# An attention and expert block on one core: turning the column maxima between two value tiles, with their result in another PSUM bank

## The chip, the cores and the metric

The kernel runs on one core of a Trainium2 chip. The metric is the device time of one execution in microseconds (us). Lower is better. Engines are named as in the profile: PE is the matrix engine, PEld its weight loads, DVE the vector engine, ACT the scalar engine, POOL the GpSimd engine, SP the engine that issues most DMAs.

## The reference, cut to what matters

```
h = layernorm(x) * (1 + ca) + sa            # x: 8 batches x 1024 rows x 256
q, k, v = h @ w_qkv                         # 16 heads of 64
attn = softmax(q @ k.T / 8, axis=-1)        # over 1024 keys, per head
x = x + ga * concat(attn @ v) @ w_o
h = layernorm(x) * (1 + cb) + sb
x = x + gb * moe(h)                         # 8 experts, 512 rows each by top-k
```

The factors sa, ca, ga, sb, cb, gb come from a small product with a conditioning vector. The change lies in the softmax of the attention: in how the maximum of the scores over the keys is found and passed on.

## The kernel before

Attention takes the first 3190 us of the span. It is cut into 128 **units** (`NSU`): a batch, a pair of heads and a half of the 1024 queries (512). A unit has 1024 keys in eight **chunks** of 128. Scores are computed transposed: keys lie on partitions, and the two heads' 512 queries each lie side by side (128 x 1024).

The loop over `g` runs four **groups** a unit (`u, gm = divmod(g, 4)`), two chunks in a group, and the instructions of each engine run in the order in which the loop writes them (`manual_schedule`). Three units are under way at once. In group g the loop writes

- `subtract` (L432, DVE): adds the negated maximum, spread over partitions by `max_spread` (L429), to two chunks of an earlier unit;
- `scores_mm` and `scores_out`: PE writes the scores of two chunks of unit u (L373), ACT copies each to SBUF (L382), DVE keeps the running maximum over chunks in `top` (L387). In the last group (`gm == 3`) one of the two subtractions comes behind these;
- the tasks "m1": projections of queries, keys (`qk_task`, L338) or values (`v_task`, L355) for later units, and at the first group of a unit `max_rows` (L416, L421);
- `exp_of` (L435, ACT), then `values_mm` for two chunks of an earlier unit (L444, PE; the group's **two value tiles**), whose sums build up in one bank over the unit's eight chunks, and `add_up` (L460, L463, POOL) for the denominators;
- in the last group `max_turn` and `split_max`: PE turns `top` in eight transposes (L394) into the tile `tt`; DVE reduces `tt` to the negated maxima (L402) and splits these into three bf16 parts in four small operations (L407 to L410), which `max_rows` turns back;
- the tasks "m2", among them the **small tasks** of the next and the previous batch: layernorm transposes, output projections, transposes of their rows.

[...] `ps_s` has two buffers of two banks each, for scores and for `tt`; they are handed out in turn, so in a last group and the next one the order is chunk 6, chunk 7, `tt`, next unit's chunk 0, its chunk 1. `ps_b` (two banks) holds the spread maximum, `ps_av` (one) the values, and `ps_m` (one, tag "mm") every projection and small task. At the very beginning `bank` hands out other banks for projections as well.

The small tasks are given groups by `free_slot`, which enters them in `taken`; with `behind` it takes last groups only:

```
def free_slot(g, behind=False):
    while g in taken or g % 4 == 0 or behind != (g % 4 == 3):
        g += 1
    taken.add(g)
```

From these calls 112 of the 128 last groups are claimed. Free are those of groups 3, 7, ... 35 (units 0 to 8) and 55, 59, ... 79 (units 13 to 19). All of them hold one "m1" task: a projection of queries or of values. In group 3 there are no value tiles yet, and `mod_rows` is written behind the turn, though it has no entry in `taken`.

Of the kernel before, what the change touches and what calls it, by code (L numbers as in the profile page):

```python
# [28 lines left out]
F32 = mybir.dt.float32  # L29
# [9 lines left out]
P = 128  # L39
# [4 lines left out]
def adaln_block(  # L44
# [77 lines left out]
    NSU = B * NP * 2  # L122
# [11 lines left out]
    ps_m = attn.enter_context(tc.tile_pool(name="ps_m", bufs=1, space=PSUM))  # L134
# [110 lines left out]
    tops, turned, rows_of, less, probs, sums, avs = {}, {}, {}, {}, {}, {}, {}  # L245
# [6 lines left out]
    def run(g, where):  # L252
        for f, args in steps.pop((g, where), ()):
            f(*args)
# [108 lines left out]
    def unit(u):  # L363
        return u // (2 * NP), u // 2 % NP, u % 2

    def scores_mm(u, c):

        b, p, h = unit(u)
        qt, kt = qks[b, p, 0], qks[b, p, 1]
        ps = ps_s.tile([P, 2, QB], F32, tag="s", name=f"s{u}_{c}")  # L370
        for j in range(2):
            r = slice(j * N, (j + 1) * N)
            nc.tensor.matmul(  # L373
                ps[:, j, :], kt[r, c * P : (c + 1) * P], qt[r, h * QB : (h + 1) * QB],
                start=True, stop=True,
            )
        return ps

    def scores_out(u, c, ps):

        probs[u, c] = work.tile([P, 2, QB], F32, tag="p", name=f"p{u}_{c}", bufs=PB)
        nc.scalar.copy(probs[u, c], ps)  # L382
        if c == 0:
            return
        if c == 1:
            tops[u] = work.tile([P, 2, QB], F32, tag="top", name=f"top{u}", bufs=1)
        nc.vector.tensor_tensor(tops[u], probs[u, 0] if c == 1 else tops[u], ps, ALU.max)  # L387

    def max_turn(u):
        top = tops.pop(u)  # L390
        turned[u] = ps_s.tile([P, 8, P], F32, tag="s", name=f"tt{u}")
        for j in range(2):
            for t in range(4):
                nc.tensor.transpose(  # L394
                    turned[u][:, 4 * j + t, :], top[:, j, t * P : (t + 1) * P], ident
                )

    def split_max(u):

        tt = turned.pop(u)  # L400
        nm = tt[:, :2, :8]
        nc.vector.tensor_reduce(nm[:, 0, :], tt, AX.X, ALU.max, negate=True)  # L402
        part = [
            parts_of[u % 2][:, :, :, i].rearrange("p t j -> p j t") for i in range(3)
        ]
        whole, rest = (nm[:, i, :].rearrange("p (j t) -> p j t", j=2) for i in range(2))
        nc.vector.tensor_copy(part[0], whole)  # L407
        nc.vector.tensor_sub(rest, whole, part[0])
        nc.vector.tensor_copy(part[1], rest)
        nc.vector.tensor_sub(part[2], rest, part[1])  # L410
# [12 lines left out]
    def max_spread(u):  # L423

        less[u] = ps_b.tile([P, 2, QB], F32, tag="less", name=f"less{u}")
        rows = rows_of.pop(u)
        for j in range(2):
            r = slice(j * N, (j + 1) * N)
            nc.tensor.matmul(less[u][:, j, :], three[r, :], rows[r, :], start=True, stop=True)  # L429

    def subtract(u, c):
        nc.vector.tensor_tensor(probs[u, c], probs[u, c], less[u], ALU.add)  # L432

    def exp_of(u, c):
        nc.scalar.activation(probs[u, c], probs[u, c], AF.Exp)  # L435

    def values_mm(u, c):
        b, p, h = unit(u)
        if c == 0:
            avs[u] = ps_av.tile([P, QB], F32, tag="av", name=f"av{u}")  # L440
        v, pT = vs[b, p // 2], probs[u, c]
        for j in range(2):
            hh = 2 * (p % 2) + j
            nc.tensor.matmul(  # L444
                avs[u][j * N : (j + 1) * N, :], v[:, c, hh * N : (hh + 1) * N], pT[:, j, :],
                start=(c == 0), stop=(c == NT - 1),
            )

    def values_out(u):
        b, p, h = unit(u)  # L450
        if h == 0:
            oTs[b, p] = work.tile([P, S], F32, tag="oT", name=f"oT{b}_{p}", bufs=2)
        nc.scalar.copy(oTs[b, p][:, h * QB : (h + 1) * QB], avs.pop(u))  # L453

    def add_up(u, i):

        pts = [probs.pop((u, 2 * i + k)) for k in range(2)]
        if i == 0:
            sums[u] = work.tile([P, 2, QB], F32, tag="acc", name=f"acc{u}")
            nc.gpsimd.tensor_tensor(sums[u], pts[0], pts[1], ALU.add)  # L460
        else:
            for pt in pts:
                nc.gpsimd.tensor_tensor(sums[u], sums[u], pt, ALU.add)  # L463
# [236 lines left out]
    taken = set()  # L700
# [5 lines that stand above are left out]
        return g  # L706
# [9 lines left out]
    for b in range(B):  # L716
# [16 lines left out]
        if b + 1 < B:  # L733
# [3 lines left out]
            for t in range(NT):  # L737
                g = free_slot(64 * (b + 1) + 19 + 4 * t, True)
# [3 lines left out]
                if t % 2:  # L742
                    g = free_slot(g + 2, True)
                    at(g, "m2", out_turn, ps_m, b, t - 1)
                    g = free_slot(g + 1)
                    at(g, "m2", out_route, ps_m, b, t - 1)
                    at(g + 1, "post", out_exp, b, t - 1)
                    g = g + 2 if g + 2 < 4 * NSU else 4 * NSU + 4
# [17 lines left out]
    with tc.manual_schedule():  # L766
# [20 lines left out]
        g = -1  # L787
        while g < 4 * NSU + LAG or steps:
            u, gm = divmod(g, 4)
            run(g, "load")  # L790
            if gm == 1 and 0 < u <= NSU:
                max_spread(u - 1)
            u1, gm1 = divmod(g - LAG + 1, 4)
            late = [(u1, 2 * gm1 + i) for i in range(2) if 0 <= u1 < NSU]

            for uc in late[: 1 if gm == 3 else 2]:
                subtract(*uc)
            if 0 <= u < NSU:
                for c in (2 * gm, 2 * gm + 1):
                    scores_out(u, c, scores_mm(u, c))  # L800
            if gm == 3 and late:
                subtract(*late[1])
            run(g, "m1")
            run(g, "post")
            for uc in late:
                exp_of(*uc)
            u1, gm1 = divmod(g - LAG, 4)
            if 0 <= u1 < NSU:
                for c in (2 * gm1, 2 * gm1 + 1):
                    values_mm(u1, c)  # L810
                if gm1 == 3:
                    values_out(u1)
                if u1 < NSU - 1 or gm1 < 2:
                    add_up(u1, gm1)
            if gm == 3 and 0 <= u < NSU:
                max_turn(u)
                split_max(u)
            run(g, "pool")
            run(g, "m2")
            g += 1  # L820
# [117 lines left out]
    with tc.tile_pool(name="search", bufs=2) as se, tc.tile_pool(  # L938
        name="pos", bufs=1
    ) as po_, tc.tile_pool(name="se_ps", bufs=2, space=PSUM) as sps, tc.tile_pool(  # L940
        name="pos_ps", bufs=1, space=PSUM
# [280 lines left out]
```

## Time and profile before

| | us |
|---|---|
| median of 3 runs (3564.46 to 3565.72) | 3565.45 |
| the profiled execution, its own time | 3568.2 |
| its span, first to last instruction | 3566.5 |
| PE busy in the span | 3435.0 |
| DVE, POOL, ACT busy in the span | 2864.9, 2657.6, 2439.2 |
| L394, turned maxima: 1024 matmuls on PE | 139.9 |
| L402, the reduction: 128 of 1.23 us each | 157.4 |
| L407 to L410, the split: 128 of each, of 0.17 to 0.19 us | 96.7 |

Busy times are sums over the span, whose parts have different limits. PE matmuls overlap, and their ends are modelled, so times on PE are better read from start to start. In the lines of a timeline the columns are start, length, engine, line, operation, output and inputs, shapes and number; brackets hold the idle time ahead and what ended it. In the lines of a table of stretches busy times of PE, PEld, DVE, ACT and POOL follow the length, and then the granted PE clock, the DMA share and GB/s. In the lines of waits the numbers are the total in us, how often, and the longest.

### The profile page before, as it was taken

Reading aid. Unit: us, or ns where it says so; the run is one execution under the profiler, and the core shown is the slowest. Engines: PE = TensorE matmul, PEld = TensorE weight load, DVE = VectorE, ACT = ScalarE, POOL = GpSimd, SP = SyncE. Lnnn points to the kernel's source line nnn. Section 1 sums busy time; section 2 is a strip of 40 time slices with the busy share of each in tenths; the row PEclk is TensorE's granted clock in tenths of the full one; section 3 lists DMA queues with packets and bytes.
Section 4 is the critical chain, followed back from the end, with each engine's and each line's share of the span. In section 5 each row is a group of like instructions: output and inputs, shape, how many; then the busy total and the mean of one; then the engine's idle time right before and its main releaser. Section 6 shows DMA issues by size and latency. Waiting matters only on the chain. (4 is left out here: it accounts for less than half of the span.)

```text
span 3566.5 us, 54197 instructions
## 1 busy us (share of the span) xinstructions
PE 3435.0 (96%) x20631; PEld 1444.8 (41%) x20631; DVE 2864.9 (80%) x3611; ACT 2439.2 (68%) x2996; POOL 2657.6 (75%) x1533
## 2 busy tenths in 40 slices
PE   8999999999999999999999999999999999993898
PEld 3333334343433434344333444334433343432566
DVE  6888888888888888888888888888888888887332
ACT  5777777777777777777777777777777777760111
POOL 2778777888888887988788877978788888881233
PEclk9999999999999999999999999999999999996899
DMA  4021012011120112111221112011211112124342
GB/s 78 13 42 31 25 40 60 29 46 46 55 56 29 50 58 56 34 40 46 63 48 35 50 52 64 25 43 45 65 52 31 47 51 57 46 80 151 94 103 42
DMA packets 190136, 185.39 MB, mean 52 GB/s; under 512 B 49308, under 2 KB 167596, under 8 KB 189748
## 3 DMA queue, kind: packets, MB, share of 16 engines
q1 hardware_dynamic: 173916, 160.54, 16.6%
q0 software_dynamic: 7168, 12.72, 1.8%
q10 hardware_dynamic: 8792, 8.67, 0.8%
q8 instruction: 162, 2.65, 0.3%
q14 instruction: 98, 0.80, 0.1%
HBM read 127.06 MB, written 63.21 MB: 53 GB/s over the span
## 5 line engine op out<-in xcount | busy, mean ns | idle before, releaser
L463 POOL TENSOR_TENSOR acc<-acc,p 128x1024 f32<-128x1024 f32 x764 | 1811.3, 2371 | 360.7 <-ACT p L435 327.5
L382 ACT COPY p<-s 128x1024 f32<-128x1024 f32 x1024 | 996.3, 1019 | 417.3 <-PE s L373 406.4
L432 DVE TENSOR_TENSOR p<-p,less 128x1024 f32<-128x1024 f32 x1024 | 1206.7, 1210 | 32.8 <-PE less L429 30.3
L387 DVE TENSOR_TENSOR top<-top,s 128x1024 f32<-128x1024 f32 x768 | 936.8, 1220 | 268.6 <-ACT p L382 228.4
L435 ACT ACTIVATE p<-p 128x1024 f32<-128x1024 f32 x1024 | 1041.7, 1057 | 73.0 <-DVE p L432 72.8
L373 PE MATMUL s<-qk,qk 64*128 64x512 f32 x4096 | 1024.3, 612 | 34.2 <-DVE parts L410 31.1
L444 PE MATMUL av<-p,v 128*64 128x512 f32 x4096 | 965.8, 592 | 1.8 <-ACT oT L453 1.8
L373 PEld LDWEIGHTS s<-qk,qk 64*128 64x128 f32 x4096 | 358.4, 186 | 527.1 <-issue 240.4
L338 PE MATMUL pq<-hT,wq 128*64 128x512 f32 x2048 | 498.4, 608 | 2.2 <-ACT hT L303 2.2
L444 PEld LDWEIGHTS av<-p,v 128*64 128x64 f32 x4096 | 281.0, 137 | 462.4 <-issue 365.8
L460 POOL TENSOR_TENSOR acc<-p,p 128x1024 f32<-128x1024 f32 x128 | 304.3, 2377 | 170.6 <-ACT p L435 170.6
L338 PEld LDWEIGHTS pq<-hT,wq 128*64 128x64 f32 x2048 | 125.2, 136 | 341.5 <-issue 210.8
L355 PE MATMUL pv<-wq,hT 128*64 128x256 f32 x2048 | 249.2, 385 | 0.0
L1142 ACT ACTIVATE h<-ph,b_sb 128x512 f32<-128x512 f32 (+1 forms) x72 | 46.1, 640 | 254.1 <-PE ph L1138 254.1
L402 DVE TENSOR_REDUCE tt<-tt 128x8 f32<-128x1024 f32 x128 | 157.4, 1230 | 68.8 <-PE tt L394 68.7
L580 PE MATMUL po<-wo,ot 128*64 128x256 f32 x1792 | 205.7, 382 | 0.0
L355 PEld LDWEIGHTS pv<-wq,hT 128*64 128x64 f32 x2048 | 135.7, 136 | 152.3 <-issue 66.5
L387 DVE TENSOR_TENSOR top<-p,s 128x1024 f32<-128x1024 f32 x128 | 155.8, 1217 | 15.0 <-ACT p L382 15.0
L394 PEld LDWEIGHTS tt<-ident,top 128*128 128x128 f32 x1024 | 109.6, 140 | 106.4 <-DVE top L387 106.4
L525 POOL TENSOR_TENSOR oT<-oT,rb 128x1024 f32<-128x1024 f32 x63 | 151.0, 2398 | 0.0
L580 PEld LDWEIGHTS po<-wo,ot 128*64 128x64 f32 x1792 | 123.6, 137 | 66.1 <-issue 9.4
L394 PE MATMUL tt<-ident,top 128*128 128x128 f32 x1024 | 139.9, 280 | 2.3 <-DVE top L387 2.3
(180 smaller groups left out, 2271.0 us busy)
## 6 DMA issues: line engine op xcount, KB each, us to landing
rb<-rden_d SPq DMA_DIRECT2D x126, 256.0 KB
oT_d<-oT SPq DMA_DIRECT2D x62, 512.0 KB
ot<-oT_d SPq DMA_DIRECT2D x56, 512.0 KB
rows_d<-row SPq DMA_DIRECT2D x64, 132.0 KB
rows_d<-gb_d SPq DMA_DIRECT2D x8, 1024.0 KB
w<-in_L_ffn_w_dram ACTq DMA_DIRECT2D x8, 1024.0 KB
w<-in_L_ffn_w_dram SPq DMA_DIRECT2D x8, 1024.0 KB
lnx<-in_L_attn_inputs_dram SPq DMA_DIRECT2D x28, 256.0 KB
```

Of the source, the lines that this page charges most:

```text
L338: nc.tensor.matmul(pq[m * N : (m + 1) * N, :], wq_of(k, a, 2 * p + m), hTs[b][:, k, sl], start=(k == 0), stop=(k == KC - 1),)
L355: nc.tensor.matmul(pv[m * N : (m + 1) * N, i, :], hTs[b][:, k, t0 : t0 + N], wq_of(k, 2, 4 * g, 4), start=(k == 0), stop=(k == KC - 1),)
L373: nc.tensor.matmul(ps[:, j, :], kt[r, c * P : (c + 1) * P], qt[r, h * QB : (h + 1) * QB], start=True, stop=True,)
L382: nc.scalar.copy(probs[u, c], ps)
L387: nc.vector.tensor_tensor(tops[u], probs[u, 0] if c == 1 else tops[u], ps, ALU.max)
L394: nc.tensor.transpose(turned[u][:, 4 * j + t, :], top[:, j, t * P : (t + 1) * P], ident)
L432: nc.vector.tensor_tensor(probs[u, c], probs[u, c], less[u], ALU.add)
L435: nc.scalar.activation(probs[u, c], probs[u, c], AF.Exp)
L444: nc.tensor.matmul(avs[u][j * N : (j + 1) * N, :], v[:, c, hh * N : (hh + 1) * N], pT[:, j, :], start=(c == 0), stop=(c == NT - 1),)
L460: nc.gpsimd.tensor_tensor(sums[u], pts[0], pts[1], ALU.add)
L463: nc.gpsimd.tensor_tensor(sums[u], sums[u], pt, ALU.add)
L580: nc.tensor.matmul(po[m * N : (m + 1) * N, :], ot[:, p, m * N : (m + 1) * N], wo[:, p, :], start=(p == 0), stop=(p == NP - 1),)
```

## The change

In the last groups that no small task has claimed, `max_turn` is written between the two value tiles instead of behind both, and `split_max` puts the negated maxima and their remainders into a tile of their own in the bank "mm", no longer into a corner of `tt`. In all other last groups the order and the tiles are as they were. In group 3 only the second part applies, since there are no value tiles.

```diff
-    def split_max(u):
+    def split_max(u, apart):
         tt = turned.pop(u)
-        nm = tt[:, :2, :8]
+        if apart:
+            nm = ps_m.tile([P, 2, 8], F32, tag="mm", name=f"nm{u}")
+        else:
+            nm = tt[:, :2, :8]
         nc.vector.tensor_reduce(nm[:, 0, :], tt, AX.X, ALU.max, negate=True)
...
             u1, gm1 = divmod(g - LAG, 4)
+            turn = gm == 3 and 0 <= u < NSU
+            alone = turn and g not in taken
             if 0 <= u1 < NSU:
                 for c in (2 * gm1, 2 * gm1 + 1):
+                    if alone and c % 2:
+                        max_turn(u)
                     values_mm(u1, c)
                 if gm1 == 3:
                     values_out(u1)
                 if u1 < NSU - 1 or gm1 < 2:
                     add_up(u1, gm1)
-            if gm == 3 and 0 <= u < NSU:
-                max_turn(u)
-                split_max(u)
+            if turn:
+                if u not in turned:
+                    max_turn(u)
+                split_max(u, alone)
             run(g, "pool")
             run(g, "m2")
```

## The prediction

> **What bounds the kernel now.** I read the page's busy shares and slices first, then the table of stretches for the granted clock, then the waits of PE, then the timeline of one affected group on PE, DVE and ACT.
>
> ```profile
> PE 3435.0 (96%) x20631; PEld 1444.8 (41%) x20631; DVE 2864.9 (80%) x3611; ACT 2439.2 (68%) x2996; POOL 2657.6 (75%) x1533
> 66.00:257.00 191.00, 181.00 (x986) 66.74 (x984) 159.28 (x169) 147.92 (x177) 143.37 (x65) 1.00 0.12 26
> 520.00:1000.00 480.00, 477.97 (x2921) 193.75 (x2919) 408.20 (x494) 356.20 (x435) 391.68 (x222) 1.00 0.19 48
> PE s L373 <- DVE parts L410: 31.1, 70, 1.3
> ```
>
> PE is busy 96% of the span, and in attention (to 3170 us) it is the engine that sets the pace: from 520 to 1000 us it rests 2 us in 480. From 66 to 257 us it rests 10 us in 191, at the same granted clock of 1.00, and the list of waits for that stretch gives all 10.0 us to one cause: scores (L373) waiting for the last instruction of the split (L410). Over the whole kernel that wait is 31.1 us in 70 times. Fifteen of these are 1.25 us each (units 1 to 8 and 13 to 19 in the timeline), 18.8 us together; the other 55 are about 0.2 us.
>
> Here is one of the fifteen, unit 19, on PE, then on DVE, then on ACT (start, length, instruction):
>
> ```profile
> 492.26 1.95 PE L355 MATMUL pv<-wq,hT 128*64 128x256 f32 x16
> 494.03 1.89 PE L444 MATMUL av<-p,v 128*64 128x512 f32 x8
> 495.85 1.10 PE L394 MATMUL tt<-ident,top 128*128 128x128 f32 x8
> 496.88 1.13 PE L373 MATMUL s<-qk,qk 64*128 64x512 f32 x4
> 499.26 1.13 PE L373 MATMUL s<-qk,qk 64*128 64x512 f32 x4 [1.25 <-DVE parts L410]
> 500.32 0.41 PE L416 MATMUL pn<-ident_b,parts 128*64 128x128 bf16 x8
> ```
>
> ```profile
> 492.62 2.55 DVE L387 TENSOR_TENSOR top<-top,s 128x1024 f32<-128x1024 f32 x2 [1.79 <-ACT p L382]
> 495.08 1.22 DVE L432 TENSOR_TENSOR p<-p,less 128x1024 f32<-128x1024 f32 x1
> 496.98 1.23 DVE L402 TENSOR_REDUCE tt<-tt 128x8 f32<-128x1024 f32 x1 [0.69 <-PE tt L394]
> ...
> 498.92 0.19 DVE L410 TENSOR_TENSOR parts<-tt,parts 128x8 bf16<-128x8 f32 x1
> ```
>
> ```profile
> 491.57 1.93 ACT L382 COPY p<-s 128x1024 f32<-128x1024 f32 x2 [0.34 <-PE s L373]
> 494.25 0.59 ACT L360 COPY v<-pv 128x512 f32<-128x512 f32 x1 [0.75 <-PE pv L355]
> ```
>
> The two score buffers rotate: chunk 6, chunk 7, turned maxima (tt), next unit's chunk 0, its chunk 1. So chunk 1 needs the buffer of tt, and the negated maxima lie in that same buffer until L410 has read them. L410 ends at 499.11, chunk 1 starts 0.15 later. PE has only chunk 0 to do meanwhile.
>
> **What the Trainium skill says.** "PSUM — Partial Sum Buffer", section "PSUM bank collisions raise a hardware error", asks to guard PSUM by bank and quadrant, not by address, readers of two engines included. The trace agrees twice: chunk 1 stays out until the small operations on a corner of the tile are over, and the maximum of chunk 6 starts at 492.62, just as the ACT copy of the same tile ends (491.57 plus half of the pair, about 492.6). The same page, "Engine vs sequencer instructions", says that matmuls start and complete in program order; so an early turn that waits holds the second value tile. "TensorE: Matmul & The Clock Gate", section "HAM oscillation — how this bites in real kernels", puts the danger at PE gaps above some 3.4 us. Here gaps are 1.25 us and the clock is 1.00 with or without them: closing them brings no clock, and I count none.
>
> **The change part by part.** It acts in 16 last groups: those that `free_slot` leaves free, groups 3 to 35 and 55 to 79. Group 3 (unit 0) has no value tiles yet, and the second modulation product follows its turn; the trace has no stall there, so it counts zero. Fifteen remain.
>
> *Stall removed.* Price it by starts, not by the reported idle: from chunk 0 to the bank transposes L416 is 500.32 − 496.88 = 3.44 us. Without a wait two chunks take 1.92 us, as in this row pair of unit 20, whose last group has an output projection as cover:
>
> ```profile
> 524.20 1.99 PE L373 MATMUL s<-qk,qk 64*128 64x512 f32 x8
> 526.12 0.41 PE L416 MATMUL pn<-ident_b,parts 128*64 128x128 bf16 x8
> ```
>
> So the stall costs 1.52 us (1.25 reported, the rest start-up of a matmul after a wait). Spacing says the same: affected units are 23.72 us apart, unit 20 takes 25.82 with a projection of 3.60, that is 22.22, or 1.50 less. The fifteen are worth 15 × 1.52 = 22.8 us.
>
> *New wait.* The turn moves ahead of the second value tile. The first ends half of 1.82 us after 494.03, at 494.94. The column maxima are ready when the pair at 492.62 ends, 495.17. From there to a waiting turn it takes 0.06 us, by the last unit, where that wait exists already:
>
> ```profile
> 3177.65 2.54 DVE L387 TENSOR_TENSOR top<-top,s 128x1024 f32<-128x1024 f32 x2
> 3180.25 1.09 PE L394 MATMUL tt<-ident,top 128*128 128x128 f32 x8 [0.59 <-DVE top L387]
> ```
>
> Turn at 495.23, PE loses 0.29 us; what is queued behind it is the second value tile, the next scores and so all of PE. Unit 18 gives the same (468.88 + 2.55 + 0.06 against 470.29 + 0.91), unit 1 gives 0.23. This cannot shrink by a lighter DVE: DVE idled 1.79 us ahead of that maximum, which hangs on the ACT copy and that on PE's own scores.
>
> *Does the stall really go?* Turn 495.23 to 496.25 (pitch 1.02), second value tile to 497.16, chunk 0 to 498.12. The reduction starts 1.13 after the turn as before, 496.36, when the addition L432 before it is just over (495.08 + 1.22 = 496.30), and ends 497.59. Plus 0.15 that is 497.74, ahead of 498.12 by 0.38. Chunk 1 doesn't wait. The split ends 3.26 us after the turn starts, as now (499.11 − 495.85), so at 498.49; the transposes L416 now come at 499.08, so they don't wait either.
>
> *The maxima in the small tasks' bank.* The reduction needs that bank free: its last user in these groups is pq or pv, copied out by ACT by 494.84 (unit 19), 1.5 us before. Next user is L416's output, which needs the split anyway. Same five DVE operations, input and output in PSUM as now, so I price them unchanged. The trace has no reduction into another bank; I bound it by nothing below and by the 0.38 us of slack above, past which it would show one for one.
>
> *A turn between two tiles that accumulate.* No row shows it. Value tiles after pv, pq or the bf16 transposes all take 1.82 a pair, so I take 0; ends −0.05 and +0.10 (what a restart costs chunk 1 now: pitch 1.06 instead of 0.96).
>
> *Behind it.* All later steps come 1.23 us earlier. ACT has 0.16 us to spare ahead of the chunk 2 copy and may slip 0.02; that copy frees nothing that PE needs for 4 us. DVE is busy 159.28 us in 8 units, 19.9 each, POOL 17.9, ACT 18.5, all under the new 22.5 of PE. No DMA is moved; SP and POOL keep their order.
>
> Sum: 22.8 − (14 × 0.29 + 0.23) = 18.5 us. The profiled execution took 3568.2 (span 3566.5) and goes to 3549.7; the median shown is 2.75 under that execution, so 3565.45 becomes **3547.0**. The bounds of the unknown terms give 13 to 21 us, 3544.5 to 3552.5.
>
> **Rivals.**
> *Held to the end (9%).* The buffer is still given back only after L410, say because the release counts the whole split. Then chunk 1 starts at 498.49 + 0.15 = 498.64 instead of 498.12, with 0.10 restart: 0.62 lost. Gain 1.52 − 0.29 − 0.62 = 0.61, times 15 is 9.2: 3556.3. Against it: the only later readers use the new tile.
> *Given back (7%).* ACT, whose slack is the smallest, or DVE with 2.6 us a unit, turns the gain into a later wait of about 0.9 us a unit; left is 5 us, 3560.5. Against it: the 520 to 1000 stretch runs at 22.2 plus tasks with the same DVE work.
> *Slower (4%): the bank of the small tasks holds the reduction.* It stands at the head of DVE's queue, with the four small operations, two additions and the next maximum behind it, and all of PE behind these. It decides from the point where the ACT copy of pq or pv ends after 496.36 + 0.38 + 1.23 − 0.10 = 497.87, 3.0 us later than now. If the copy came only behind the next unit's chunk 0 copy (498.11 + 1.01 + 0.59 = 499.7), chunk 1 would start at 501.1, 1.8 us later than today: +27 us, 3592. Against it: ACT idles 0.75 us ahead of that copy.
> *It doesn't do what it says (2%).* Another set of groups is touched and the stalls stay: 3565. For the fifteen speaks that exactly those without a claimed slot stall 1.25 us.
>
> **How the numbers follow.** The forecast itself has 78%. Its own span 3544 to 3552.5 holds about 75 in 100; reaching to the first rival, 3556.5, takes in 8 in 10 and a little more. Faster or slower means by more than 0.2% (7 us), about what a measurement of this kernel can tell from no change: faster are the forecast, the first rival and a part of the second, 0.90; same 0.06; slower 0.04.
>
> **What would show it.** Right: "scores waiting for L410" falls from 31.1 to about 12 us with 0.2 the longest; a new wait of turn for column maxima of about 0.2 to 0.3 us in 15 places; affected units 22.5 apart; DVE's idle ahead of the reduction near 0.1 there. Wrong: waits of 0.4 us or more at L410 in those units (first rival), a reduction that waits for ACT (third), or a turn that waits over 0.9 us.

## The result, and the profile after

The change makes the kernel faster: 3546.82 us (median of 5, 3545.16 to 3549.73) against 3564.94 for the kernel before on the same chip. The ratio is 0.995, interval 0.9939 to 0.9961, that is 17.8 us, between 13.9 and 21.7; the medians lie 18.1 apart. The profiled execution took 3549.73 us with a span of 3548.0, 18.5 less than before.

The busy shares, and the stretch of units 1 to 8 in the table of stretches:

```profile
PE 3434.0 (97%) x20631; PEld 1444.1 (41%) x20631; DVE 2863.3 (81%) x3611; ACT 2437.4 (69%) x2996; POOL 2657.8 (75%) x1533
66.00:248.00 182.00, 180.76 (x986) 66.33 (x984) 158.59 (x169) 147.26 (x178) 143.62 (x64) 1.00 0.09 27
```

The same 986 matmuls keep PE busy for 180.8 us (181.0 before), in 182 us instead of 191. No engine has less to do; PE rests 1.2 us where it rested 10. The granted clock is 1.00, as before.

The waits of PE in the changed kernel (total, times, longest; the split's last line is now L413):

```profile
PE s L373 <- DVE parts L413: 12.3, 55, 0.2
...
PE tt L394 <- DVE top L387: 4.6, 17, 1.0
```

The fifteen long waits for the split are gone, and the 55 short ones in other groups stand. The turn, which waited 2.3 us in 3 places before, waits 4.6 in 17.

Unit 19 again, PE first, then DVE:

```profile
475.80 1.95 PE L355 MATMUL pv<-wq,hT 128*64 128x256 f32 x16
477.57 1.03 PE L447 MATMUL av<-p,v 128*64 128x512 f32 x4
478.76 1.09 PE L394 MATMUL tt<-ident,top 128*128 128x128 f32 x8 [0.15 <-DVE top L387]
479.78 1.08 PE L447 MATMUL av<-p,v 128*64 128x512 f32 x4
480.79 1.99 PE L373 MATMUL s<-qk,qk 64*128 64x512 f32 x8
482.71 0.41 PE L419 MATMUL pn<-ident_b,parts 128*64 128x128 bf16 x8
```

```profile
476.15 2.55 DVE L387 TENSOR_TENSOR top<-top,s 128x1024 f32<-128x1024 f32 x2 [1.79 <-ACT p L382]
478.62 1.22 DVE L435 TENSOR_TENSOR p<-p,less 128x1024 f32<-128x1024 f32 x1
479.96 1.23 DVE L405 TENSOR_REDUCE nm<-tt 128x8 f32<-128x1024 f32 x1
```

Both chunks of scores run in one piece, 1.92 us from 480.79 to the transposes at 482.71. From the first value tile to those transposes it is 5.14 us, where it was 6.29 (500.32 − 494.03). The reduction now starts 0.12 us after the addition ends (479.84); before, DVE idled 0.69 us ahead of it. The turns of units 18 and 19 are 22.60 us apart; they were 23.74.

### The profile page after: what moved, and what is told of

Its sections match the earlier page's. It is cut to its first block, busy times and chain, and to the rows that moved or that the text cites. A ratio compares the mean times of both kernels' runs of the same rounds, so it can differ in the third digit from the quotient of the medians.

```text
span 3548.0 us, 54197 instructions
## 1 busy us (share of the span) xinstructions
PE 3434.0 (97%) x20631; PEld 1444.1 (41%) x20631; DVE 2863.3 (81%) x3611; ACT 2437.4 (69%) x2996; POOL 2657.8 (75%) x1533
## 5 line engine op out<-in xcount | busy, mean ns | idle before, releaser
L373 PE MATMUL s<-qk,qk 64*128 64x512 f32 x4096 | 1020.3, 611 | 15.4 <-DVE parts L413 12.3
L405 DVE TENSOR_REDUCE tt<-tt 128x8 f32<-128x1024 f32 x112 | 137.7, 1230 | 56.4 <-PE tt L394 56.2
```

The source lines that it names most:

```text
L373: nc.tensor.matmul(ps[:, j, :], kt[r, c * P : (c + 1) * P], qt[r, h * QB : (h + 1) * QB], start=True, stop=True,)
```

## The experiments

The changed kernel rests on two edits at once, so I first made each alone. The theory: the bank decides when chunk 1 may start, the early turn shifts the chain forward and pays for it with a new wait. Each median below was taken beside the kernel before on the same chip (3566.09 us for the first four runs, 3566.00 for the last two). I compare its ratio with the 0.995 of the change, and the spacing of the turns of units 18 and 19 in the traces, where differences under 0.1 us can be read.

**The early turn alone.**

```diff
-                split_max(u, alone)
+                split_max(u, False)
```

> The turn stays between the two value tiles in the 15 groups, the maxima go back to a corner of tt. Theory (two parts: the bank decides when chunk 1 may start, the early turn only shifts the chain): in unit 19 of the changed kernel the split ends at 482.09, chunk 1 could start at 481.75 and now must wait to 482.24, plus 0.10 restart: 0.59 us lost in each of 15 groups, 3546.8 + 8.9 = 3555.7; chunk 1 waits about 0.4 to 0.5 us at the last split operation again, the turn still waits some 0.16 us. Rival A (the early turn alone is the gain, the bank is incidental): 3547. Rival B (the bank alone is the gain, the early turn costs 0.38 a group): slower than 3565, about 3571.

Measured: 3556.28, ratio 0.9973 (0.9963 to 0.9984), which is 8 us above the change (8.9 expected). On PE in unit 19:

```profile
487.14 1.13 PE L373 MATMUL s<-qk,qk 64*128 64x512 f32 x4
488.51 1.13 PE L373 MATMUL s<-qk,qk 64*128 64x512 f32 x4 [0.24 <-DVE parts L413]
489.57 0.41 PE L419 MATMUL pn<-ident_b,parts 128*64 128x128 bf16 x8
```

Chunk 1 waits for the split again. From chunk 0 to the transposes it is 2.43 us against 1.92: 0.51 lost (0.59 expected), of which the bracket tells 0.24. The reported wait was to be 0.4 to 0.5; that number I had worked out from starts, and it must not be looked for in the bracket. Rivals A and B both fall: the early turn alone is a gain, but only about half of the whole.

**The bank alone.**

```diff
-                    if alone and c % 2:
+                    if False and c % 2:
```

> The maxima have their own bank in the 16 groups, the turn stays behind both value tiles. Theory: no wait of the turn (0.28 a group saved against the change) and no dearer value tile, but the reduction ends at 498.21 in the old timeline and chunk 1 could start at 497.84; it starts at 498.36, 0.52 late plus 0.10 restart: 1.52 - 0.62 = 0.90 gained of each of 15 groups, 13.5 us, 3551.4. The wait named is the reduction, not the last split operation. Rival A (early turn alone is the gain): 3565. Rival B (bank alone): 3542 to 3547.

Measured: 3552.20, ratio 0.9961 (0.9948 to 0.9975); about 4 us above the change, 4.6 expected. The waits of PE name what was expected, the reduction:

```profile
PE s L373 <- DVE nm L405: 5.0, 15, 0.3
```

```profile
482.81 1.13 PE L373 MATMUL s<-qk,qk 64*128 64x512 f32 x4
484.27 1.13 PE L373 MATMUL s<-qk,qk 64*128 64x512 f32 x4 [0.34 <-DVE nm L405]
485.33 0.41 PE L419 MATMUL pn<-ident_b,parts 128*64 128x128 bf16 x8
```

From chunk 0 to the transposes it is 2.52 us, 0.60 over the undisturbed 1.92 (0.62 expected). Rivals A and B fall here too. The wait now ends with the reduction and no longer with the split, so it is the bank that decides which of the two chunk 1 waits for. The turns of units 18 and 19 are 22.83 us apart. So of the 1.14 us a unit that both edits gain together, the bank alone gives 0.91 and the early turn alone 0.63 (spacing 23.11). The two overlap: each takes away a part of one and the same stall.

**The turn's new wait taken away.** In the sixteen groups DVE takes the maximum of chunk 6 before ACT copies it, and ACT copies chunk 7 first:

```diff
+    def scores_swap(u):
+        pss = [scores_mm(u, 6), scores_mm(u, 7)]
...
+        nc.vector.tensor_tensor(tops[u], tops[u], pss[0], ALU.max)
+        nc.scalar.copy(probs[u, 7], pss[1])
+        nc.vector.tensor_tensor(tops[u], tops[u], pss[1], ALU.max)
+        nc.scalar.copy(probs[u, 6], pss[0])
```

> The change, and in the same 16 groups DVE takes the maximum of chunk 6 ahead of ACT's copy of it, and ACT copies chunk 7 first. Theory (the turn's new wait hangs on ACT copy, then two maxima): chunk 6 is done about 0.9 us earlier on DVE, chunk 7's maximum follows its copy, the column maxima are ready some 0.37 us earlier, the wait of 0.28 us is gone: 14 x 0.28 + 0.22 = 4.1 us, 3542.7. Rival C (the wait is cover for something as late, such as the buffer of tt, which now waits for ACT's later copy of chunk 6): no change, 3547, with the turn waiting for ACT.

Measured: 3545.55, ratio 0.9944 (0.993 to 0.9957). Against 0.995 that is 2 us (4.1 expected), within the intervals; by the times alone it isn't shown. The trace shows it (the turn is L403 here, values L456, transposes L428):

```profile
474.10 1.03 PE L456 MATMUL av<-p,v 128*64 128x512 f32 x4
475.06 1.09 PE L403 MATMUL tt<-ident,top 128*128 128x128 f32 x8
476.08 1.08 PE L456 MATMUL av<-p,v 128*64 128x512 f32 x4
477.09 1.99 PE L373 MATMUL s<-qk,qk 64*128 64x512 f32 x8
```

The turn's bracket is empty. Units are 22.37 us apart, 0.23 closer than in the change; fifteen of these are 3.4 us. So the wait hung on the ACT copy, as argued, and the later copy of chunk 6 holds nothing up; rival C falls. But the first value tile now takes 0.96 us with no wait behind it, where I had counted 0.91. Of the 1.19 us from first tile to turn in the change, 0.23 were wait and 0.96 the tile.

**The early turn where there is nothing to win.** In the 56 groups with an output projection too:

```diff
+            ahead = turn and g in proj
...
-                    if alone and c % 2:
+                    if (alone or ahead) and c % 2:
```

Here `proj` holds the slots of `out_proj`.

> The change, and the turn also between the value tiles in the 56 last groups that hold an output projection, where no score chunk waited before (maxima stay in tt there). Prices the early turn by itself: theory, 0.28 wait for the column maxima plus 0.10 on the value tile behind it, nothing to win: 56 x 0.38 = 21 us slower than the change, 3568. Rival D (the early turn is free, since a value tile is only swapped): 3547.

Measured: 3562.62, ratio 0.999 (0.9982 to 0.9999): about 14 us lost against the change, not 21. The early turn has a price, so rival D falls, but my price for most of these groups was too high:

```profile
602.03 1.03 PE L447 MATMUL av<-p,v 128*64 128x512 f32 x4
603.22 1.09 PE L394 MATMUL tt<-ident,top 128*128 128x128 f32 x8 [0.17 <-DVE top L387]
604.25 1.08 PE L447 MATMUL av<-p,v 128*64 128x512 f32 x4
605.15 3.62 PE L583 MATMUL po<-wo,ot 128*64 128x256 f32 x32
608.71 1.99 PE L373 MATMUL s<-qk,qk 64*128 64x512 f32 x8
610.62 0.41 PE L419 MATMUL pn<-ident_b,parts 128*64 128x128 bf16 x8
```

8.59 us from the first tile to the transposes, where the change takes 8.36 in this group (601.74 to 610.10): 0.23 lost. So it is in 54 of the 56 groups, 12.6 us together. In the last two (units 125 and 126) the turn waited for the column maxima already, 1.0 and 0.7 us; moved forward it waits 1.88 and 1.55, and these two groups lose 2.55 and 0.76 us. From the first unit's transposes to the last unit's, the trace is thus 15.9 us longer than that of the change; the part behind them, where nothing was changed, happens to be 2.0 us shorter. Ahead of a projection the second value tile takes 0.90 us and the projection 3.56 (3.60 behind a turn); ahead of scores the tile takes 1.01.

**The early turn behind a short cover.** The same edit for the 56 groups whose small task is a short row of transposes (`ahead = turn and g in taken and g not in proj`).

> The change, and the turn also between the value tiles in the 56 last groups that hold a short small task (layernorm transposes or row transposes, 1.02 us), where chunk 1 waits 0.22 us for the last split operation (0.40 by start pitch and 0.10 restart); maxima stay in tt there. Theory: each gains 0.50 and pays 0.38, net 0.12, about 6.6 us: 3540. Rival D (early turn is free): 27 us, 3519. Rival E (the short task already covers, nothing to win, early turn only costs): 3568.

Measured: 3534.17, ratio 0.9911 (0.9898 to 0.9925), 14 us below the change; 6.6 were expected. The list of PE's waits no longer holds scores waiting for the split. One such group:

```profile
649.73 1.03 PE L447 MATMUL av<-p,v 128*64 128x512 f32 x4
650.93 1.09 PE L394 MATMUL tt<-ident,top 128*128 128x128 f32 x8 [0.17 <-DVE top L387]
651.95 1.08 PE L447 MATMUL av<-p,v 128*64 128x512 f32 x4
652.86 1.04 PE L312 MATMUL ptx<-ident,lnx 128*64 128x128 f32 x16
653.83 1.99 PE L373 MATMUL s<-qk,qk 64*128 64x512 f32 x8
655.75 0.41 PE L419 MATMUL pn<-ident_b,parts 128*64 128x128 bf16 x8
```

6.02 us against 6.28 in the change (651.28 to 657.56): 0.26 a group instead of the 0.12 that I had worked out. So it is in 54 of the 56; units 41 and 127, where the turn waits 0.50 and 1.45 us, lose 0.08 and 0.35, and the sum is 13.8 us. The difference to my 0.12 is the second value tile (0.91, not 1.01) and the transposes behind it (0.97, not 1.02). Rivals D and E fall.

**Both together.** The previous run, and with it the order "maximum first" of the third run in the same 72 last groups: the sixteen of the change and these 56. In 71 of them the turn is early; group 3 has no value tiles.

> As the run before, and in all 72 groups with an early turn DVE takes the maximum of chunk 6 ahead of ACT's copy, and ACT copies chunk 7 first. Theory: takes the turn's wait of about 0.28 us away in some 70 groups, 19.6 us below the run before, about 3520. Rival C (the turn then waits for ACT's later copy of chunk 6, which holds its buffer): same as the run before, 3540.

Measured: 3518.58, ratio 0.9867 (0.9852 to 0.9882). That is 16 us under the previous run (19.6 expected), 30 us under the change and 47 under the kernel before. In the trace nearly every one of the 71 groups is about 0.23 us shorter than there, and the sum is 16.2 us. Rival C falls once more.

## Why the prediction was right, point by point

*Which groups, and the stall.* Right. The fifteen long waits were the ones predicted and are gone: 31.1 less 12.3 is 18.8 us of reported wait. Chunk 0 to the transposes takes 1.92 us, not 3.44, so each was worth 1.52. Only the reason given for the 0.27 us that the bracket leaves out was half right: 0.10 is the slower start of chunk 1 (1.06 us to the transposes instead of 0.96), and 0.17 is the modelled end of chunk 0, which the profile puts 1.13 us after its start, where an undisturbed chunk 1 would start after 0.96.

*The buffer comes free at the reduction.* Right; the first rival (held to the end) is shut out by unit 19, where chunk 1 doesn't wait, and the run with the bank alone names the reduction as what chunk 1 waits for. The run with the early turn alone is just the case that this rival describes: it gained 0.63 us a unit where the rival had 0.61.

*The new wait.* The time from the first value tile to the turn was right, its parts were not. I took half of a pair of value tiles, 0.91 us, for one tile, and 0.29 for the wait. The turn came 1.19 us after the first tile, the forecast was 1.20. The run without that wait shows 0.96 for the tile, so the wait itself is 0.23 (0.17 in unit 1). The sign named for it, 0.2 to 0.3 us in 15 places, holds only by starts: the list of waits shows 14 places of 0.15 to 0.17, and none for unit 1.

*A turn between two accumulating tiles.* This is the term that was mis-sized: I took 0, with an upper end of 0.10, and it was 0.10, at the edge of what I had allowed. The second value tile lasts 1.01 us to the start of the scores where I counted 0.91; the last section says why. A unit thus gains 6.29 − 5.14 = 1.15 us, not 1.23, and fifteen 17.2, not 18.5.

*Then why does the span fall by exactly 18.5?* Partly by luck. The first turn of the kernel lies 0.5 us earlier in the profile after (46.33 against 46.79), ahead of any changed group. The last one comes 17.6 earlier (3162.64 against 3180.25), so 17.1 are due to what lies between; the remaining 0.9 us comes behind the last turn, where nothing was changed. Neither is a gain of the edit; the runs of the change themselves differ by 4.6 us. For the same reason the measured median says no more than that the gain is near 18 us; that it lies 0.2 us from the forecast is luck as well.

*The reduction into the other bank.* Right: 1.23 us, as in place, and no wait for ACT. The rival on the slower side had its point at a copy 3.0 us later; the copy of pv still begins 0.22 us after the first value tile (477.79), as before (494.25 against 494.03).

*Behind it.* Right: apart from that of the turn, PE shows no new wait in attention with the shorter units, and the next stretches run at the pace that they had (PE 477.99 busy in 480 us from 520 to 1000, 477.97 before).

*The clock.* Right: it was 1.00 in the stretch with gaps of 1.25 us and is 1.00 without them. The bound of 3.4 us that the prediction took from the Trainium skill ("TensorE: Matmul & The Clock Gate", section "HAM oscillation — how this bites in real kernels") is neither reached nor tested by these stretches.

## What to carry to other kernels

When an engine waits for a buffer, ask which reader is the last, and whether that reader needs the large tile at all: here two rows of eight columns, the maxima and their remainders, kept two PSUM banks busy through four small operations. Price a stall from start to start in a group with it and one without it; the bracket told 1.25 of 1.52 us, and 0.24 of 0.51 in another run. Two cures of one stall don't add up (0.91 and 0.63 gave 1.14 us), and an instruction moved forward pays wherever its own input is just in time, so look at what its input hangs on before looking for another place.

## What the runs showed of the hardware that was not expected

Where PE goes on to instructions of another shape (rows*columns in the lines, 128*64 for value tiles), a step gets longer. In the kernel before, weight loads inside a pair of value tiles come every 0.43 us, but the last step to the turn (128*128) is longer:

```profile
494.46 0.14 PEld L444 LDWEIGHTS av<-p,v 128*64 128x64 f32 x2 [0.29 <-issue]
494.89 0.14 PEld L444 LDWEIGHTS av<-p,v 128*64 128x64 f32 x2 [0.29 <-issue]
495.85 0.86 PEld L394 LDWEIGHTS tt<-ident,top 128*128 128x128 f32 x8 [0.81 <-DVE top L387]
```

From 494.89 two steps of 0.43 lead to 495.75, and the turn starts at 495.85, though its input had been there since 495.17. So the pair lasts 4 × 0.43 plus 0.10, its 1.82 us.

Matmul by matmul, the same trace shows that this is no accident of the turn. Where PE doesn't wait, the last step of value tiles takes 0.53 us (0.57 and 0.67 in two of 476 places) where it goes on to scores (64*128), turns (128*128) or denominators (128*32), and 0.43 in all 28 places where it goes on to the small products `pl`, which have the same shape. The projections of queries, of that shape too, take 0.43 ahead of value tiles and 0.53 ahead of the turn of group 3 (44.97 to 46.79). Entering 128*64 from another shape costs less: the first step is then 0.48.

This explains the times of the experiments. A value tile alone is 0.86. The first, ahead of a turn, takes 0.96; the second, behind a turn, takes 0.86 + 0.05 + 0.10 = 1.01 ahead of scores, and 0.91 ahead of a projection or of small transposes of the same shape. These, entered from their own shape, then take 0.05 less themselves (3.56 instead of 3.60, 0.97 instead of 1.02). So the price that I put at nothing could have been read from the kernel before. The shape was not varied by itself, but another bank or another kind of instruction doesn't account for the step: from a projection of queries to a value tile the bank changes too, and the small transposes are transposes like the turn.
